# A fused normalize, convolve and project block on one core: how early products, weight rows and the low-rank preparation are ordered

## The chip, the cores and the metric

The kernel runs on one core of a Trainium2 chip. The core has TensorE (PE in the profile, its weight loads PEld), VectorE (DVE), ScalarE (ACT), GpSimd (POOL) and SyncE (SP), which here only issues transfers. Each engine works through its own instruction list in order. The metric is the device time of one execution in microseconds (us); the median of three runs is given.

## The reference

The input x has 4 x 1024 rows of 2048 numbers. A small vector c per batch gives, through a 2048 x 12288 weight, six rows per batch: shift, scale and gate for each of two halves.

```
mod = (silu(c) @ wmod).reshape(4, 6, 1, -1)        # sa, ca, ga, sb, cb, gb
h = layernorm(x) * (1 + ca) + sa
x = x + ga' * (causal_conv(h, K) + D * h)           # K: 2048 taps from a 64-state model
h = layernorm(x) * (1 + cb) + sb
x = x + gb' * (h @ W.T + bias + sum_e w_e * (h @ A_e.T) @ B_e.T)
```

The gates ga', gb' keep their sign and are at least 0.25 in size. The convolution runs along the 2048 features of a row. It is linear in h, so the convolution of the shift sa is the same for every row of a batch and can be added afterwards.

## The kernel before, in words

**Stages.** The 4096 rows are 32 row tiles of 128. In the first phase (to about 880 us) each row tile is loaded (conv_load), normalized, transposed, split into two f16 parts and multiplied with a Toeplitz form of K (conv_prep, conv_mm). In the second phase (from about 880 us) 16 units of 256 rows are multiplied with the merged weight, by a Strassen-like scheme of seven products (ffn_unit, L745). The merged weight W + low-rank part is made during the first phase: prep_lora scales the low-rank factors A and B and splits B into lbh and lbl; merge, eight times, makes the low-rank products lps (L481), adds them to W on VectorE (L483) and writes the pieces to DRAM.

**Modulation.** wmod is read as six sections of 16 weight rows, each row 1 MB (mod_load, L312), each followed by four matmuls of 512 columns into one PSUM bank (mod_mm, L317; named modps). Section 1 (scale) comes first, then 0 (shift), then 2 (gate); sections 4, 3 and 5 come later, among the merges. Sections 1 and 0 alternate between pools of two and three buffers, section 2 has three buffers.

**Early tiles.** Tiles 0 and 1 are transposed without the shift, and the products of tiles 0 to 2 (EARLY = 3) are made before the gate exists. The generator rows issues the weight rows of sections 0 and 2 between these products; pace is told the columns of each group of three products and takes a row for every ROWC of them. The convolved shift is made by shift_conv (16 small f32 matmuls, gsp) and added to tiles 0 and 1 by shift_add (L409, L415): 16 matmuls against the identity (in two passes each, 32 records) put it on all partitions, four at a time. When the gate is there, gate_tile spreads it over the partitions (gps L669, gat L670), and conv_late (L645, L646) gates the three early tiles on VectorE; conv_post stores them (L651) and takes the sums for the second normalization (ScalarE, L655).

**Order.** The program text is traced by a framework that places instructions on each engine by its own estimate of when they are ready; a block under tc.issue_after(ins) is queued behind ins on that instruction's engine. From tile 3 on, PLAN lists at which points of a tile the normalization of the next tile (N), its statistics (T, F), the storing of the last (P) and steps of other work (S) are traced. A step takes one piece of the generator rest, which yields the pieces of mer (prep_lora, then the merges) and, after every second piece, one row of the modulation sections left. In the kernel before, the first piece, which is the whole of prep_lora, is taken before tile 3, and further steps start at tile R0 = 5, nine per tile:

```
    stats(EARLY + 1)
    nxt = prep(EARLY + 1)
    take(nxt, 1)
    next(fill)
    post = None
```

Buffers that matter: y has three buffers (EARLY), the transposed pieces t two, the transposes in PSUM (tp) two banks, the products five banks; one buffer, tagged we, holds in turn the factor A (la), the factor B (lb) and the weight tile of a merge.

Of the kernel before, what the change touches and what calls it, by code (L numbers as in the profile page):

```python
# [1 line left out]

# [10 lines left out]
F32 = mybir.dt.float32  # L13
# [6 lines left out]
MUL, ADD, SUB = ALU.mult, ALU.add, ALU.subtract  # L20
# [4 lines left out]
P = 128  # L25
D = 2048
NB = 4
NC = D // P
# [6 lines left out]
class Net:  # L35
# [354 lines left out]
    def shift_conv(self, pool):  # L390

        nc, v = self.nc, self.nc.vector
        sa = pool.tile([P, NC], F32, tag="sae", name="sae")
        v.tensor_scalar(sa, self.sa[:, :, 0], self.es, self.hinv[:, 0:1], MUL, MUL)
        ps = self.tps.tile([P, NC], F32, tag="t", name="gsp")
        for m in range(NC):
            nc.tensor.matmul(
                ps[:, m:NC], self.kb[:, ds(P * m, P)], sa[:, 0 : NC - m],
                start=(m == 0), stop=(m == NC - 1), skip_group_check=True,
            )  # L400
        self.gsc = self.kpool.tile([P, NC], F32, tag="gsc", name="gsc")
        v.tensor_copy(self.gsc, ps)

    def shift_add(self, ys):
        nc, v = self.nc, self.nc.vector
        for q in range(4):
            ps = self.tps.tile([P, 4, P], F32, tag="t", name="gsb")
            for c in range(4):
                nc.tensor.matmul(  # L409
                    ps[:, c], self.gsc[:, 4 * q + c : 4 * q + c + 1].to_broadcast([P, P]), self.ident,  # L410
                    start=(c == 0), stop=(c == 3), skip_group_check=True,
                )
            for y in ys:
                sl = ds(512 * q, 512)
                v.tensor_tensor(y[:, sl], y[:, sl], ps.rearrange("p c t -> p (c t)"), ADD)  # L415

    def prep_lora(self, pool, tmp):
        nc, v, io = self.nc, self.nc.vector, self.io
        ws = pool.tile([P, 2, 2], F32, tag="lws", name="lws")  # L420
        for i, n in enumerate(("coeffs", "scales")):
            x = io[n]
            for k in range(2):
                src = bass.AP(tensor=x.tensor, offset=x.offset + 8 * k, ap=[[1, 8], [0, 16], [1, 1]])
                nc.sync.dma_start(out=ws[:, i, k : k + 1], in_=src)
        a = tmp.tile([P, 2, D], F32, tag="we", name="la")
        nc.sync.dma_start(out=a, in_=io["A"].rearrange("c p k h d -> p c k (h d)"))

        am = pool.tile([P, 2], F32, tag="lam", name="lam")
        av = a.rearrange("p k d -> p (k d)").rearrange("p (c k d) -> p k c d", c=HC, k=2)  # L430
        for k in range(2):
            nc.scalar.activation(av[:, k], av[:, k], AF.Square, accum_out=am[:, k : k + 1])
        nc.scalar.activation(am, am, AF.Sqrt)
        sa, ia = self.pow2(pool, am, 2, "lsa")
        wt = pool.tile([P, 2], F32, tag="lwt", name="lwt")
        v.tensor_tensor(wt, ws[:, 0, :], ws[:, 1, :], MUL)
        v.tensor_tensor(wt, wt, ia, MUL)
        self.lsa = sa
        b = tmp.tile([P, 2, D], F32, tag="we", name="lb")
        nc.scalar.dma_start(out=b, in_=io["BfT"].rearrange("(k p) o -> p k o", p=P))  # L440
        b4 = pool.tile([P, 4], F32, tag="lb4", name="lb4")
        for k in range(2):
            nc.scalar.activation(b[:, k], b[:, k], AF.Copy, scale=wt[:, k : k + 1])
            for h in range(2):
                j = tmp.tile([P, 1024], F32, tag="wct", name="lsq")
                i = 2 * k + h
                nc.scalar.activation(j, b[:, k, ds(1024 * h, 1024)], AF.Square, accum_out=b4[:, i : i + 1])
        bm = pool.tile([P, 1], F32, tag="lbm", name="lbm")
        v.tensor_reduce(bm, b4, AX.X, ADD)
        nc.scalar.activation(bm, bm, AF.Sqrt)  # L450
        sb, self.linv = self.pow2(self.cst, self.allmax(pool, bm, 1, "lbm"), 1, "lsb")
        self.bh = pool.tile([P, 2, D], F16, tag="lbh", name="lbh")
        self.bl = pool.tile([P, 2, D], F16, tag="lbl", name="lbl")
        for k in range(2):
            nc.scalar.activation(b[:, k], b[:, k], AF.Copy, scale=sb)
            nc.scalar.copy(self.bh[:, k], b[:, k])
            v.tensor_tensor(self.bl[:, k], b[:, k], self.bh[:, k], SUB)
        self.winv = self.const("winv", [P, NC])
        self.wcd = self.dram.tile([2, 7, P, HC, 2, 512], F16, tag="wcd", name="wcd")
# [128 lines left out]
                v.tensor_tensor(lo[:, sl], src, hi[:, sl], SUB)  # L588
            yield

    def conv_mm(self, pl, hs, x, tick, early, pace=lambda n: None):
        nc, v = self.nc, self.nc.vector
        hc, hs = hs
        y = pl["y"].tile([P, D], F32, tag="y", name="y")
        yv = y.rearrange("p (j e t) -> p j e t", e=2, t=P)
        if not early:
            gv = self.gat.rearrange("p (j e t) -> p j e t", e=2, t=P)
        sums = pl["sm"].tile([P, 2], F32, tag="sums", name="sums")

        def family(ps, f, q, first):  # L600
            pf = ps.rearrange("p j t -> p (j t)")
            last = 4 * q + 3
            for i in range(last + 1):
                o = P * max(0, i - 4 * q)
                k0 = P * max(0, 4 * q - i)
                for x, z in ((0, 0), (0, 1), (1, 0)):
                    h = hs[x][:, i] if f == 0 else hc[x][:, 2 * i + 2 - f]
                    nc.tensor.matmul(  # L608
                        pf[:, o:512], h, self.kf[f][z][:, ds(k0, 512 - o)],
                        start=first, stop=(i == last and (x, z) == (1, 0)), skip_group_check=True,  # L610
                    )
                    first = False
                if i == 3 and q == 1:
                    tick()
                pace(3 * (512 - o))

        for q in range(2):
            jj = slice(4 * q, 4 * q + 4)
            pa = self.acc.tile([P, 4, P], F32, tag="a", name="ya")
            family(pa, 0, q, True)  # L620
            qs = pl["t"].tile([P, 4, P], F32, tag="qs", name="qs")
            nc.scalar.copy(qs, pa)  # L622
            tick()
            pb = self.acc.tile([P, 4, P], F32, tag="a", name="yb")
            family(pb, 2, q, True)
            v.tensor_tensor(yv[:, jj, 1, :], pb, qs, ADD)
            if not early:
                v.tensor_tensor(yv[:, jj, 1, :], yv[:, jj, 1, :], gv[:, jj, 1, :], MUL)
            tick()
            family(pa, 1, q, False)  # L630
            sl = ds(1024 * q, 1024)
            if early:
                nc.scalar.copy(yv[:, jj, 0, :], pa)
            else:
                v.tensor_tensor(yv[:, jj, 0, :], pa, gv[:, jj, 0, :], MUL)  # L635
                v.scalar_tensor_tensor(y[:, sl], y[:, sl], 1.0, x[:, sl], MUL, ADD, accum_out=sums[:, q : q + 1])  # L636
            tick()
        return y, sums
# [169 lines left out]
LPLAN = ("LL", "LL", "LL", "LL", "L", "0", "")  # L808
R0 = 5
WM, WMS = 3, 2  # L810
ROWC = 3700
EARLY = 3
X0 = 11
LEFT0 = 30
# [12 lines left out]
def net(ctx: ExitStack, tc: tile.TileContext, io):  # L827
    nc = tc.nc
    k = Net(ctx, tc, io)
# [10 lines left out]
    pl = {}  # L840
# [25 lines left out]
        yield  # L866

    def merges():
        with tc.issue_after(k.lastw.ins):
            k.prep_lora(pl["lora"], pl["mrg"])  # L870
        yield
        for c in range(HC):
            yield from k.merge(pl["lora"], pl["mrg"], c)

    mer = merges()

    def take(g, n):
        for _ in range(n):
            next(g, None)
# [10 lines left out]
    xs, hs, sts, ys = {}, {}, {}, {}  # L890
# [14 lines left out]
    n = 0  # L905
# [19 lines left out]
    def pace(n):  # L925

        cols[0] += n
        while cols[0] >= ROWC:
            cols[0] -= ROWC
            take(rows, 1)  # L930

    for r in range(2):
        load(r + 2)
# [1 line left out]
    stats(2)  # L935
    take(prep(2), 9)
    k.shift_conv(msm)
    k.shift_add([ys[r][0] for r in range(2)])
    st.close()
    for name in ("lora", "mrg"):  # L940
        pl[name] = pool(right, "p1" + name, 1, "right")
# [15 lines left out]
    fill = rest()  # L957
    p2l = ExitStack()
    pr, wc, lf = {}, {}, {}
# [21 lines left out]
    def next_left(u):  # L981
# [2 lines left out]
        lf[u] = {}  # L984
        return k.left(pr, u, lf[u])

    def step():
        if r >= R0 and "w" not in pr and next(fill, 0) == 0:
            early()

    stats(3)
# [12 lines left out]
    stats(EARLY + 1)  # L1004
    nxt = prep(EARLY + 1)
    take(nxt, 1)
    next(fill)
    post = None
    for r in range(EARLY, 32):
        if EARLY + 2 < r + 2 < 32:  # L1010
# [5 lines left out]
        if r == LEFT0:  # L1016
            while "w" not in pr:
                step()
            lgen = next_left(0)
# [19 lines left out]
        y = k.conv_mm(pl, hs.pop(r), xs[r], tick, False)  # L1039
# [12 lines left out]
    for q in range(2):  # L1052
# [5 lines left out]
        for u in range(NU):  # L1058
            b = u // 4
            if u % 4 == 0:  # L1060
                ts_ = []
                for i in range(2):
                    t = pr["g"].tile([P, 2, 512], F32, tag=f"gb{i}", name=f"gb{i}")
# [76 lines left out]
```

## Time and profile before

| | |
|---|---|
| median of 3 runs | 2149.5 us (2147.16 to 2152.45) |
| the profiled execution | 2147.28 us, of which span 2145.5 us |
| TensorE busy | 2077.9 us, 97% of the span |
| VectorE, ScalarE, GpSimd busy | 1309.7, 927.8, 5.1 us |
| mean granted TensorE clock | 0.986 |
| moved by DMA | 483.05 MB, mean 225 GB/s |

The span runs from the first to the last instruction. In the lists of the profile each row is a slice or stretch of it; busy time of an engine in a stretch can be compared with the stretch's length. A wait is named by who waited and which instruction was the last to end before it could go on; a wait on several signals carries only one name. A matmul of 512 f16 columns shows as 0.38 us but the next can start 0.216 us later. f32 matmuls are two records each.

### The profile page before, as it was taken

To read this page: it belongs to the slowest core of one execution; us is meant where nothing else is said; L and a number is where in the kernel's file an instruction comes from. 1 tells how busy PE (TensorE), PEld (TensorE's weight loads), DVE (VectorE), ACT (ScalarE), POOL (GpSimd) and SP (SyncE) were. 2 spreads that over 40 slices of the span, in tenths; PEclk is the share of its full clock that TensorE was granted. 3 is DMA by queue.
4 is the path that set the end of the run, shared out by engine and by line. 5 is a ranking of instruction groups with operands and counts; after the bars stand their busy time and mean duration, and the time that the engine had idled before them with its cause. 6 is when DMAs were issued, how large, how long until landed. Compare 5 with 4: busy or idle time off the path is not lost.

```text
span 2145.5 us, 28479 instructions
## 1 busy us (share of the span) xinstructions
PE 2077.9 (97%) x11144; PEld 1027.8 (48%) x11144; DVE 1309.7 (61%) x2356; ACT 927.8 (43%) x1697; POOL 5.1 (0%) x16
## 2 busy tenths in 40 slices
PE   6997899999999999999999999999999999999998
PEld 2343455545545555554545545545444444444444
DVE  6636888998989999666565565565433323332323
ACT  1344776677757777655554454455200000000000
POOL 0000000000000000000000000000000000000000
PEclk8998899999999999999999999999999999999999
DMA  9979457786777554297465565564794545555542
GB/s 395 359 248 342 178 193 280 283 309 253 280 282 285 187 177 167 104 377 276 175 246 192 182 241 186 197 240 180 269 353 164 185 157 165 170 164 166 176 157 69
DMA packets 127061, 483.05 MB, mean 225 GB/s; under 512 B 13577, under 2 KB 13721, under 8 KB 95951
## 3 DMA queue, kind: packets, MB, share of 16 engines
q1 hardware_dynamic: 126192, 477.55, 61.1%
q10 hardware_dynamic: 526, 2.63, 0.4%
q8 instruction: 87, 1.43, 0.3%
q0 software_dynamic: 208, 1.06, 0.1%
q14 instruction: 48, 0.39, 0.1%
HBM read 325.89 MB, written 155.30 MB: 224 GB/s over the span
## 4 chain that ended last, share of the span: by engine, by line
PE 65%; DVE 13%; ACT 8%; issue 2%; DMA 2%; DVEq 0%; ACTq 0%
PE fZ L745 23%; PE fX L745 15%; PE fY L745 15%; PE ya L608 5%; PE tp L695 3%; PE yb L608 2%; ACT t L577 2%; DVE wch L509 2%; ACT x L655 2%; DVE st L535 2%; DVE y L636 1%; DVE hc L588 1%; ACT we L500 1%; PE lps L481 1%; DVE n L552 1%
## 5 line engine op out<-in xcount | busy, mean ns | idle before, releaser
L745 PEld LDWEIGHTS <-lf 128*128 128x128 f16 x5376 | 526.0, 98 | 620.5 <-issue 0.9
L745 PE MATMUL fZ<-w,lf 128*128 128x512 f16 x2304 | 514.1, 379 | 0.6 <-ACT p L753 0.6
L745 PE MATMUL fY<-w,lf 128*128 128x512 f16 x1536 | 342.1, 379 | 0.0
L745 PE MATMUL fX<-w,lf 128*128 128x512 f16 x1536 | 342.1, 379 | 0.0
L608 PEld LDWEIGHTS <-hc 128*128 128x128 f16 x2304 | 216.1, 98 | 204.0 <-issue 38.8
L763 DVE TENSOR_TENSOR xo<-xo,gb 128x512 f32<-128x512 f32 x128 | 87.6, 689 | 235.1 <-DMA xo<-x1d 222.5
L608 PE MATMUL ya<-kh,hc 128*128 128x512 f16 (+3 forms) x768 | 191.3, 327 | 5.5 <-ACT qs L622 5.1
L608 PE MATMUL ya<-kh,hs 128*128 128x512 f16 (+3 forms) x768 | 194.0, 328 | 0.9 <-DVE kh L284 0.6
L608 PE MATMUL yb<-kh,hc 128*128 128x512 f16 (+3 forms) x768 | 191.7, 327 | 2.1 <-DVE we L483 1.2
L577 ACT ACTIVATE t<-tp,sa,ca 128x128 f32<-128x128 f32 x480 | 186.4, 468 | 12.4 <-PE tp L573 12.1
L753 ACT COPY p<-fZ 128x512 f32<-128x512 f32 x64 | 37.3, 583 | 293.1 <-PE fZ L745 275.3
L608 PEld LDWEIGHTS <-hs 128*128 128x128 f16 x1152 | 107.2, 98 | 108.6 <-issue 31.4
L697 ACT ACTIVATE gt<-tp,sb,cb 128x256 f32<-128x256 f32 x256 | 125.0, 576 | 62.5 <-PE tp L695 60.9
L753 ACT COPY p<-fX 128x512 f32<-128x512 f32 x32 | 18.8, 586 | 305.8 <-PE fX L745 241.7
L317 PE MATMUL modps<-wm,sct 128*32 128x512 f32 x768 | 115.2, 660 | 19.9 <-DMA wm<-in_wmod 12.6
L608 PE MATMUL ya<-kl,hs 128*128 128x512 f16 (+3 forms) x384 | 125.7, 327 | 1.9 <-DVE kl L285 1.9
L608 PE MATMUL ya<-kl,hc 128*128 128x512 f16 (+3 forms) x384 | 125.6, 327 | 0.0
L608 PE MATMUL yb<-kl,hc 128*128 128x512 f16 (+3 forms) x384 | 125.5, 327 | 0.0
L573 PE MATMUL tp<-ident,n 128*128 128x128 f32 x512 | 80.7, 283 | 28.4 <-ACT t L577 16.0
L768 DVE TENSOR_TENSOR fin<-fX,gb 128x512 f32<-128x512 f32 x32 | 22.1, 691 | 127.1 <-PE fX L745 127.0
L588 DVE TENSOR_TENSOR hc<-t,hc 128x512 f16<-128x512 f32 x128 | 87.5, 683 | 12.0 <-ACT hc L587 11.8
L481 PE MATMUL lps<-lbh,lac 128*128 128x512 f16 x256 | 86.1, 379 | 0.2 <-DVE y L635 0.2
(262 smaller groups left out, 2222.9 us busy)
## 6 DMA issues: line engine op xcount, KB each, us to landing
wm<-in_wmod SPq DMA_DIRECT2D x96, 1024.0 KB
lfd<-lf SPq DMA_DIRECT2D x112, 512.0 KB
lf<-lfd SPq DMA_DIRECT2D x112, 512.0 KB
x<-in_x SPq DMA_DIRECT2D x32, 1024.0 KB
x1d<-y SPq DMA_DIRECT2D x32, 1024.0 KB
x<-x1d SPq DMA_DIRECT2D x32, 1024.0 KB
xo<-x1d SPq DMA_DIRECT2D x128, 256.0 KB
out<-xo SPq DMA_DIRECT2D x128, 256.0 KB
```

Source lines behind the costliest of these rows:

```text
L317: self.last = self.nc.tensor.matmul(self.modps[32 * g : 32 * g + 32, :], self.sct[:, j].rearrange("p r b -> p (r b)"), w[:, ds(512 * g, 512)],
L481: nc.tensor.matmul(ps, la[:, x, k, h], y[:, k, osl], start=(n == 0), stop=(n == 5))
L509: v.tensor_tensor(hl[:, :, 1, :], tv, hl[:, :, 0, :], SUB)
L573: nc.tensor.transpose(tp[:, k], n[:, ds(P * (c0 + k), P)], self.ident)
L577: nc.scalar.activation(t[:, k], tp[:, k], AF.Identity, bias=self.sa[:, c, b : b + 1], scale=self.ca[:, c, b : b + 1],)
L588: v.tensor_tensor(lo[:, sl], src, hi[:, sl], SUB)
L608: nc.tensor.matmul(pf[:, o:512], h, self.kf[f][z][:, ds(k0, 512 - o)], start=first, stop=(i == last and (x, z) == (1, 0)), skip_group_chec ...
L695: nc.tensor.transpose(tp[:, c, r], xs[r][:, ds(P * (c0 + c), P)], self.ident)
L697: nc.scalar.activation(t[:, c0 + c], tp[:, c], AF.Identity, bias=self.sb[:, c0 + c, b : b + 1], scale=self.cb[:, c0 + c, b : b + 1],)
L745: nc.tensor.matmul(ps[name], lf[i][:, k, x, :], wc[i][k // 4][:, k % 4, y, :], start=(first and n == 0), stop=(n == 3 * HC - 1), skip_grou ...
L753: nc.scalar.copy(t, ps[name])
L763: v.tensor_tensor(x, x, self.gbias[:, h], ADD)
```

## The change

1. conv_mm: a group of three products is now traced inside the block that pace returns, and pace returns tc.issue_after(k.last.ins), where k.last is the last matmul of the weight rows so far. So each group of an early tile stands behind the weight row that was due before it. For tile 3 and later pace is an empty block. ROWC goes from 3700 to 3000 columns.
2. shift_conv now copies the 128 x 16 result, transposes it to 16 x 128, copies it and stores it in DRAM; shift_add reads it back on all partitions by one DMA of 1 MB into the buffer of the gate tile, both on GpSimd's queue, and adds it to each tile with one VectorE instruction over 2048 columns.
3. prep_lora has seven yields. With the modulation rows between, it takes the first piece (before tile 3) and nine steps; in tiles 3 and 4 every second step is now taken. The first piece is queued behind the last weight row's load.

```
-        self.gsc = self.kpool.tile([P, NC], F32, tag="gsc", name="gsc")
-        v.tensor_copy(self.gsc, ps)
-    def shift_add(self, ys):
-        for q in range(4):
-            ps = self.tps.tile([P, 4, P], F32, tag="t", name="gsb")
-            for c in range(4):
-                nc.tensor.matmul(ps[:, c], self.gsc[:, 4*q+c : 4*q+c+1].to_broadcast([P, P]), self.ident, ...)
-            for y in ys:
-                v.tensor_tensor(y[:, sl], y[:, sl], ps.rearrange("p c t -> p (c t)"), ADD)
+        col = pool.tile([P, NC], F32, tag="gsc", name="gsc")
+        v.tensor_copy(col, ps)
+        pt = self.tps.tile([NC, P], F32, tag="t", name="gst")
+        nc.tensor.transpose(pt, col, self.ident)
+        row = pool.tile([NC, P], F32, tag="gsr", name="gsr")
+        v.tensor_copy(row, pt)
+        self.gsd = self.dram.tile([NC, P], F32, tag="gsd", name="gsd")
+        nc.gpsimd.dma_start(out=self.gsd, in_=row)
+    def shift_add(self, pool, ys):
+        g = pool.tile([P, D], F32, tag="gat", name="gsb")
+        self.nc.gpsimd.dma_start(out=g, in_=self.gsd.rearrange("c t -> (c t)").partition_broadcast(P))
+        for y in ys:
+            self.nc.vector.tensor_tensor(y, y, g, ADD)
...
     def prep_lora(self, pool, tmp):
         nc.sync.dma_start(out=a, in_=io["A"].rearrange("c p k h d -> p c k (h d)"))
+        yield
...
         nc.scalar.activation(am, am, AF.Sqrt)
+        yield
...
         nc.scalar.dma_start(out=b, in_=io["BfT"].rearrange("(k p) o -> p k o", p=P))
+        yield
...
+        yield
         bm = pool.tile([P, 1], F32, tag="lbm", name="lbm")
         v.tensor_reduce(bm, b4, AX.X, ADD)
         nc.scalar.activation(bm, bm, AF.Sqrt)
+        yield
...
             nc.scalar.copy(self.bh[:, k], b[:, k])
+            yield
...
-    def conv_mm(self, pl, hs, x, tick, early, pace=lambda n: None):
+    def conv_mm(self, pl, hs, x, tick, early, pace=lambda n: nullcontext()):
-                for x, z in ((0, 0), (0, 1), (1, 0)):
+                with pace(3 * (512 - o)):
+                    for x, z in ((0, 0), (0, 1), (1, 0)):
...
-                pace(3 * (512 - o))
...
-ROWC = 3700
+ROWC = 3000
...
     def merges():
-        with tc.issue_after(k.lastw.ins):
-            k.prep_lora(pl["lora"], pl["mrg"])
-        yield
+        yield from k.prep_lora(pl["lora"], pl["mrg"])
...
     def pace(n):
             take(rows, 1)
+        return tc.issue_after(k.last.ins)
...
+    calls = [0]
     def step():
-        if r >= R0 and "w" not in pr and next(fill, 0) == 0:
+        calls[0] += 1
+        if r < R0 and calls[0] % 2:
+            return
+        if "w" not in pr and next(fill, 0) == 0:
             early()
...
-    next(fill)
+    with tc.issue_after(k.lastw.ins):
+        next(fill)
```

## The prediction

> **What bounds the kernel now.** I read the busy shares and the slices first, then the busy time by stretch, then waits and chain inside the worst stretch, then TensorE's instructions there. From the page of the kernel before:
>
> ```profile
> PE 2077.9 (97%) x11144; PEld 1027.8 (48%) x11144; DVE 1309.7 (61%) x2356; ACT 927.8 (43%) x1697; POOL 5.1 (0%) x16
> PE   6997899999999999999999999999999999999998
> DVE  6636888998989999666565565565433323332323
> PEclk8998899999999999999999999999999999999999
> ```
>
> TensorE fills the span; 67.6 us of it are idle, mostly in slices 1 and 4 to 5. So only idle time or the lower clock of those slices can be won. By stretch (length, busy PE, PEld, DVE, ACT, POOL, clock, DMA share, GB/s):
>
> ```profile
> 132.00:144.00 12.00, 12.00 (x78) 8.78 (x81) 5.15 (x12) 3.65 (x9) 0.00 (x0) 0.72 0.44 153
> 144.00:171.00 27.00, 27.00 (x182) 11.51 (x177) 10.53 (x20) 10.49 (x26) 0.00 (x0) 1.00 0.89 298
> 171.00:202.00 31.00, 26.87 (x152) 12.41 (x151) 22.79 (x49) 12.76 (x18) 0.00 (x0) 0.94 0.93 354
> 202.00:227.00 25.00, 5.97 (x29) 3.25 (x27) 20.89 (x52) 22.28 (x32) 0.36 (x1) 0.58 0.86 332
> 227.00:252.00 25.00, 25.00 (x152) 14.74 (x151) 23.20 (x57) 17.86 (x46) 0.00 (x0) 0.94 0.44 169
> 252.00:880.00 628.00, 614.25 (x3797) 328.13 (x3796) 562.67 (x1181) 444.02 (x920) 0.42 (x1) 1.00 0.64 236
> ```
>
> From 202 to 227 TensorE works 6 us of 25, at a clock of 0.58, while VectorE and ScalarE are full. TensorE in it, with the idle time before each piece:
>
> ```profile
> 202.17 0.22 PE L608 MATMUL ya<-kh,hc 128*128 128x128 f16 x1
> 213.38 1.97 PE L573 MATMUL tp<-ident,n 128*128 128x128 f32 x8 [10.99 <-DVE lsb_i L54]
> 216.10 1.93 PE L317 MATMUL modps<-wm,sct 128*32 128x512 f32 x8 [0.75 <-DMA wm<-in_wmod]
> 224.52 1.11 PE L573 MATMUL tp<-ident,n 128*128 128x128 f32 x4 [6.49 <-ACT t L577]
> ```
>
> The first wait is for row tile 4's normalized n (L552 runs 211.99 to 213.33; lsb_i is the last VectorE name before it). The second is for ScalarE to take transposes out of PSUM, and the chain says what ScalarE did instead:
>
> ```profile
> 215.70 3.79 ACT lb L455 x2
> 219.49 3.59 ACT lbh L456 x2
> 223.07 1.74 ACT t L577 x5
> ```
>
> So the low-rank preparation stands in front of tile 4's preparation. VectorE is behind for another reason: the late gating of tiles 0 to 2 (L645, L646) starts only at 180.56.
>
> **What the Trainium skill says.** "TensorE: Matmul & The Clock Gate", Part 1, gives half clock after an idle window of about 3.4 us; the trace agrees (a 384-column product takes 0.32 us of issue at 138, 0.165 normally). "DMA: Bandwidth & Descriptors", Issuing engines are not separate DMA queues: transfers from all engines share the same 16 DMA engines; so the new broadcast competes with the weight rows. The same page, Anatomy of one DMA, has about 2.0 us fixed plus bytes over 436 GB/s, 4.4 us for 1 MB; under load this trace has 5.2 us for the 8 KB kd store and 10.0 us for the 1 MB kb load on GpSimd's queue, and I use those. "Perfetto Trace Analysis", Optimization Strategy, advises interleaving regimes with different bounds, which is what the spread preparation is.
>
> **The change part by part.** Instruction orders are those of the two built programs. I compare three places.
>
> *(a) Up to the end of tile 2's products.* Before, from 64.3 us: 3 tiles x 41,472 columns x 0.2158/512 us = 52.4; 31 weight rows x 1.00 = 31.0; 48 transposes x 0.115 = 5.5; the shift's convolution gsp 4.7; its broadcast gsb 0.57 + 1.66 + 1.9 = 4.1 (32 passes); 0.5 else. Sum 98.2, waits 1.9 + 1.2, and 4 for half clock from 132 to 144: 169.6; the trace has it at 171.4. The new form takes gsb away and adds one transpose (0.2): -4. VectorE does two adds of 2,048 (2 x 2.3, as lbl) where it did eight of 512 (2 x 2.48): nothing.
>
> A row every 3,072 columns costs TensorE 1.3 + 1.0 = 2.3 us, the transfer 2.58 at the 407 GB/s of the stretch from 20 to 40 us. The row order is strict now, so rows could starve TensorE. Between the 64th us and the last row are 31 rows, 2 x tiles and the broadcast, 34 x 2.58 = 87.7, less some 2.5 rows already there: 81. TensorE needs about 88 to the same place, since transposes and gsp lie between rows: covered on average, 1 to 3 us lost to local order. If the cover is gone it is 0.3 us a row, 9 in all.
>
> The broadcast's wait: behind its add on VectorE stand tile 3's subtractions, behind these ScalarE's next transposes and the copy qs of tile 2, and for that TensorE's third family. Landing is 1 + 0.5 + 5.2 + 0.5 + 10.0 = 17 us after the transpose, the copy is done at 23; TensorE arrives there after 8 rows, 23,000 columns and 16 transposes = 19.5, or 23.5 with the half clock seen at this place. Bounds: 0 to 4 us; I take 1. Tile 2's products end at 167 to 169 against 171.4.
>
> *(b) The gate.* The last weight row comes 2,304 + 29,952 columns = 13.6 us before that end, where before it came after the start of tile 3. The gate's 3.5 us of VectorE and Abs are hidden in it. The broadcast of the gate (gps, 4.0) follows directly, so the first late gating starts near 170, not 180.56: 10.5 us earlier.
>
> *(c) From there to the first merge product.* VectorE's work, counted from the order: 17 of 1,024 (1.22), 15 of 512 (0.61), 10 hc and 10 hs (0.60, 0.34), 11 sm (0.34), 16 stats (0.62), 3 n (1.26), 2 gate halves still to come (0.76), 2 lbl (2.25), some 60 small (7): about 70 us. The same count of before gives 64, and the trace 71.0 (180.56 to 251.57), so 7 were waits. After: 170 + 70 + 3 to 7 = 243 to 247, with 6 us of work done more than before had: worth 251.57 + 6 - 245 = 12 us.
>
> TensorE over the same piece: tile 3 ends near 191 with its three rows; n of tile 4 comes at 197.5 (VectorE's sum up to it), an idle 6 us; transposes are no longer behind L455 and L456, and tile 4's products start near 203 instead of 227.5. They run, fed by VectorE, to 224; tile 5's first family, transposes and three rows to 229.5. Then the moved wait: the first low-rank product needs lbh, whose two scalings (1.99 each) and casts (1.89) wait for the scale at about 229 on VectorE, so lbh comes at 234.8: 5.3 us idle. TensorE is at 239.5 where before it was at 257, with two weight rows (2 us) more behind it: 17.5 us, less some 4 for half clock after the idle: 13.5. ScalarE's 19.5 us of preparation (2 x 1.9, 2 x 1.99, 4 x 1.06, 2 x 1.99, 2 x 1.89) are neither fewer nor more; they lie under tiles 3 and 4.
>
> What is late next is the merge's weight tile: it shares the buffer of lb, so its load can't start before lbl is done at about 239; it lands 5 to 7 us later, when VectorE gets there (246). Price without that cover: what it is late. From tile 5 on there are 182 steps left in both programs, in the same order, so what is gained is kept; VectorE at 90% there (562.67 of 628) can hold back a part, which is why I go no higher.
>
> Sum: 12 by VectorE, 13.5 by TensorE, and a little recovered: 14 us. The profiled execution took 2147.28, span 2145.5 and 1.8 around; less 14 it is 2133.3. The median of the runs lies 2.2 higher: 2135.5.
>
> **Rivals.** *The larger gain:* lbh is in time, or the clock doesn't fall at 191: 14 + 5 + 4 = 23 us, 2126. For it: ScalarE has waits in (c) that my sum fills; against: VectorE's count.
>
> *The stall only moves:* ScalarE has 12 us of its own a tile and 10 of preparation against some 19.5 us of TensorE a tile; if in-order waits cost as much as the 25 us block, only gsb's 4 us remain: 2145. For it: VectorE is full either way; against: 10.5 us of earlier start are VectorE time that lies idle before (it works 10.53 of the 27 us from 144 to 171).
>
> *Slower:* strict rows make the early stage wait for transfers. Place: rows 19 to 48, with three buffers in the last sixteen. 31 MB at 300 GB/s would take 108 us instead of 88, all of it on TensorE: 14 - 20 = 6 lost, 2155.5, more if slower; it decides below about 370 GB/s. For it: 298 and 310 GB/s are all this stage shows; against: TensorE asked for no more then, and 0 to 60 us ran at 395 to 407.
>
> **How the numbers follow.** Forecast 0.58 (alone 2130 to 2142), larger gain 0.17, moved stall 0.14, slower 0.11. A measurement tells 0.3%, 6.4 us, from no change. Faster: 0.58 + 0.17 = 0.75; same 0.14; slower 0.11. The range 2124 to 2149 reaches to the moved stall and the larger gain, and leaves out the slower case and the far end of the larger gain; it holds the broadcast's 0 to 4, the rows' 0 to 9 and the moved wait's 0 to 10.
>
> **What would show it.** The 25 us stretch should shrink to 6 or so idle before tile 4's transposes, with their releaser n and not L455; no wait of the weight rows above 3 us in sum between 64 and 150; first late gating near 170; a new wait of a few us of the first low-rank product for lbh. It is wrong if weight rows wait for their DMA at every row, if TensorE waits on qs while VectorE waits for gsb, or if the first merge comes near 250 as before.

## The result and the profile after

The changed kernel takes 2142.6 us in the median of six runs (2140.33 to 2145.74), beside 2151.5 us for the kernel before on the same chip (now six runs, with the three of the table above among them): a ratio of 0.9960, 95% interval 0.9946 to 0.9974. It is 8.9 us faster, where 14 were forecast.

The two profiled executions show less of this than the medians do. The one after took 2145.74 us (span 2143.8), the longest of its six; the one before, 2147.28 us, is among the shortest of its own. The two traces differ by 1.5 us. They are good for what waits for what, and the size is left to the medians.

The busy shares and TensorE's slices, from the page of the changed kernel:

```profile
PE 2080.1 (97%) x11113; PEld 1026.8 (48%) x11113; DVE 1308.9 (61%) x2351; ACT 927.3 (43%) x1697; POOL 6.2 (0%) x18
...
PE   6897999999999999999999999999999999999998
```

TensorE's idle time is 63.7 us against 67.6. Its busy time rose by 2.2 us, although the 32 records of the shift's broadcast (4.1 us) are gone. The gap in slices 4 and 5 is smaller, not closed. The same stretches as before (length, busy PE, PEld, DVE, ACT, POOL, clock, DMA share, GB/s):

```profile
132.00:144.00 12.00, 11.64 (x67) 6.68 (x65) 3.60 (x9) 4.06 (x11) 1.09 (x2) 0.72 0.62 225
144.00:171.00 27.00, 26.55 (x180) 11.84 (x177) 13.36 (x21) 10.89 (x26) 0.00 (x0) 1.00 0.89 325
171.00:202.00 31.00, 22.99 (x112) 11.39 (x110) 16.87 (x32) 16.12 (x21) 0.00 (x0) 0.89 0.68 244
202.00:227.00 25.00, 20.45 (x124) 11.40 (x124) 24.56 (x62) 16.75 (x37) 0.00 (x0) 0.86 0.92 342
227.00:252.00 25.00, 22.55 (x143) 12.18 (x142) 23.50 (x58) 21.01 (x40) 0.35 (x1) 0.93 0.48 177
252.00:880.00 628.00, 615.55 (x3774) 328.14 (x3773) 564.33 (x1185) 442.14 (x918) 0.41 (x1) 1.00 0.65 237
```

From 202 to 227 TensorE now works 20.45 us instead of 5.97. But from 171 to 202 it lost 3.9 us, from 227 to 252 another 2.4, and VectorE, which I had wanted full from 171 on, works 16.87 us there instead of 22.79. TensorE's waits in that piece, from its list of instructions:

```profile
191.86 0.59 PE L614 MATMUL ya<-kh,hc 128*128 128x512 f16 x1 [6.75 <-ACT qs L627]
214.20 1.97 PE L578 MATMUL tp<-ident,n 128*128 128x128 f32 x8 [3.28 <-DVE n L557]
...
218.55 0.61 PE L614 MATMUL ya<-kh,hs 128*128 128x512 f16 x1 [0.52 <-ACT hs L592]
247.11 0.38 PE L486 MATMUL lps<-lbh,lac 128*128 128x512 f16 x1 [2.45 <-ACT lbh L460]
```

The transposes of tile 4 wait 3.28 us for n, no longer behind the scaling and casting of B. In their place stands a wait of 6.75 us inside tile 3's products, for ScalarE's copy out of PSUM (qs). The chain of waits from 157 us says why:

```profile
157.68 15.88 DMA la<-in_A
173.66 3.90 ACT la L432 x4
177.60 11.66 DMA lb<-in_BfT
189.34 2.01 ACT lb L445
191.38 0.45 ACT qs L627
191.86 7.67 PE ya L614 x33
```

A's load, the squares of A, B's load and the first scaling of B follow each other, and tile 3's copy stands behind that scaling in ScalarE's list. ScalarE sits idle until B has landed, and from 185.1 us on TensorE with it. (L445 was L443 in the kernel before, where it stood behind the stores' squares and didn't wait.)

### The profile page after: what moved, and what is told of

It is laid out like the page before. It is cut to its first block, busy times and chain, and to the rows that moved or that the text cites. A ratio compares the mean times of both kernels' runs of the same rounds, so it can differ in the third digit from the quotient of the medians.

```text
span 2143.8 us, 28420 instructions
## 1 busy us (share of the span) xinstructions
PE 2080.1 (97%) x11113; PEld 1026.8 (48%) x11113; DVE 1308.9 (61%) x2351; ACT 927.3 (43%) x1697; POOL 6.2 (0%) x18
## 4 chain that ended last, share of the span: by engine, by line
PE 70%; DVE 13%; DMA 8%; ACT 6%; issue 2%; SPq 0%; ACTq 0%; DVEq 0%
PE fZ L750 23%; PE fY L750 15%; PE fX L750 15%; PE ya L614 6%; PE yb L614 3%; PE tp L700 2%; PE modps L317 2%; DMA wm<-in_wmod 2%; PE lps L486 2%; ACT x L660 2%; DVE hc L593 1%; DVE wch L514 1%; ACT t L582 1%; DVE st L540 1%; DVE y L641 1%
## 5 line engine op out<-in xcount | busy, mean ns | idle before, releaser
L593 DVE TENSOR_TENSOR hc<-t,hc 128x512 f16<-128x512 f32 x128 | 87.4, 683 | 10.5 <-ACT hc L592 9.9
```

## The experiments

Two theories stood at the start; the forecast had put the gain down to both of their causes. **Theory A**: the preparation in nine steps is what gains. **Theory B**: the denser, strict weight rows gain, by an earlier gate, and the nine steps only move the wait. Times are medians, with that of the kernel before on the same chip beside them; "alone" means on the kernel before. The ratio is the one on record, with its 95% interval. It isn't the quotient of the two medians; the two differ by up to 0.0012, so a difference between two ratios that is smaller than this says nothing.

**1. The nine steps alone.** The kernel before with the seven yields of prep_lora, the step counter and the queueing of the first piece:

```
-        with tc.issue_after(k.lastw.ins):
-            k.prep_lora(pl["lora"], pl["mrg"])
-        yield
+        yield from k.prep_lora(pl["lora"], pl["mrg"])
```

> The kernel before with the low-rank preparation in nine steps alone. Theory A (the preparation standing in front of tile 4 was the cost, and spreading it is the gain): 8 to 12 us faster than before, with the idle time of TensorE ahead of tile 4's transposes down from 11 + 6.5 us to under 8. Theory B (the gain comes from the earlier gate, so from the denser rows; the preparation only moves its wait): within 3 us of before, with a new wait on ScalarE for lb's transfer of some 10 us in the place of the old one.

Measured: 2150.0 us beside 2149.1, ratio 1.0002 (0.9992 to 1.0012). No gain. What the nine steps were to do does happen: tile 4's first product starts at 215.3 us instead of 227.3. But the preparation is only pushed back: the first scaling of B goes from 201.9 to 218.4, its last cast ends at 255.1 instead of 223.1, and the first low-rank product comes at 253.4, after the 250.1 of before. The wait for B's transfer that Theory B expected is not there: that scaling starts without waiting. TensorE's waits from 171 to 310 us in this kernel:

```profile
PE tp L579 <- DVE r_v L69: 9.3, 1, 9.3
...
PE lps L487 <- ACT lbh L461: 1.8, 1, 1.8
```

TensorE's idle time falls from 67.6 to 62.6 us, its busy time rises from 2077.9 to 2082.2; where those 4.3 us of slower work lie I did not settle.

**2. The pacing alone.** pace returns the queueing block, ROWC 3000:

```
-ROWC = 3700
+ROWC = 3000
     def pace(n):
             take(rows, 1)
+        return tc.issue_after(k.last.ins)
```

> The kernel before with early products behind their weight rows and a row every 3000 columns, alone. Theory A: nothing gained, 0 to 4 us slower, since TensorE waits on rows (about 3 us more idle between 80 and 160 us than before, as in the changed kernel) and the gate that comes earlier meets the undivided preparation on ScalarE. Theory B: 6 to 9 us faster, the late gating starting near 170 instead of 180.6.

Measured: 2141.7 us beside 2149.1, ratio 0.9959 (0.9945 to 0.9974): as much as the whole change gains, by this part alone. The time is Theory B's, its reason isn't: late gating starts at 179.5, not near 170. So what the pacing does had to be asked anew (experiments 5 to 7).

**3. The shift's broadcast through DRAM alone.**

```
-            for c in range(4):
-                nc.tensor.matmul(ps[:, c], self.gsc[:, ...].to_broadcast([P, P]), self.ident, ...)
+        self.nc.gpsimd.dma_start(out=g, in_=self.gsd.rearrange("c t -> (c t)").partition_broadcast(P))
```

> The kernel before with the shift's convolution broadcast through DRAM alone. If TensorE's 32 passes (4.1 us) were on the path: 3 to 4 us faster. If VectorE and ScalarE set the end of this stage (the 25 us block comes at the same time): under 1 us. If the wait for the broadcast holds up tile 3's preparation: slower by 1 to 3 us, with a wait of VectorE for gsb.

Measured: 2152.6 us beside 2149.1, ratio 1.0013 (1.0005 to 1.0021): slightly slower. TensorE's waits from 171 to 252 us:

```profile
PE tp L572 <- DVE lsb_i L52: 19.4, 1, 19.4
PE modps L317 <- DMA wm<-in_wmod: 4.1, 1, 4.1
```

The wait at tile 4's transposes was 11.0 us in the kernel before and is 19.4 here: TensorE gets there with less to do and waits for the same n (213.8 against 212.0). All its waits in this stretch sum to 28.7 us against 23.3 before, so the 4.1 us saved ahead of a wait that VectorE and ScalarE set went into waiting. Why it is 5.4 and not 4.1 stays open; the wait of VectorE for the broadcast (gsb) that could have made it slower does not appear.

**4. The changed kernel without the wait for B.** The scaling of B queued behind tile 3's last copy out of PSUM:

```
+            with self.tc.issue_after(self.lastqs.ins):
                 nc.scalar.activation(b[:, k], b[:, k], AF.Copy, scale=wt[:, k : k + 1])
```

> The changed kernel with the scaling of lb queued behind tile 3's last copy qs on ScalarE, so that the wait for lb's transfer (10.7 us) no longer stands in front of the copies that TensorE needs and the sums that VectorE needs. Theory A: the waits of 6.75 us on TensorE and 6.7 us on VectorE go, 4 to 7 us faster than the changed kernel, 13 to 16 faster than before. Rival C (VectorE's queue sets this stage in any case): within 2 us of the changed kernel, 7 to 11 us faster than before.

Measured: 2134.2 us beside 2149.1, ratio 0.9924 (0.9909 to 0.9939), some 8 us below the changed kernel. The 6.75 us wait is gone, the first scaling of B runs at 189.94 without waiting, n of tile 4 comes at 203.5 instead of 212.8 and the first low-rank product at 241.2 instead of 247.1. So the wait for B costs the changed kernel about 8 us, more than the 5 us that are missing from the forecast. Late gating starts at 178.66 in this kernel, only 1.9 us earlier than in the kernel before: its gain of some 15 us came without the early gate that the forecast had counted on.

**5. The pacing with a late preparation.** If the pacing gains because A's squares start earlier, holding them back must take the gain away. The squares get a bias of zero that VectorE makes after the gate; the rows stay early:

```
+            self.zero = pool.tile([P, 1], F32, tag="zero", name="zero")
+            v.tensor_scalar(self.zero, t[:, D - 1 : D], 0.0, None, MUL)
-            nc.scalar.activation(av[:, k], av[:, k], AF.Square, accum_out=am[:, k : k + 1])
+            nc.scalar.activation(av[:, k], av[:, k], AF.Square, bias=self.zero, accum_out=am[:, k : k + 1])
```

> The early products' new pacing alone, but the first squaring of the low-rank preparation on ScalarE is given an operand that VectorE makes only after the gate (one more instruction of 128x1, about 0.15 us): the weight rows stay early, the chain of the preparation (squares of A, load of B, scalings, casts) starts about 10 us later, as in the kernel before. Theory P (the pacing's gain is that the last weight row frees ScalarE's preparation 10 us sooner, so that tile 4's transposes are taken out sooner): the gain is gone, 2147 to 2151 us, with the squaring of A at 181 to 184. Theory Q (the gain is in TensorE's rows or in the gate themselves): 2140 to 2144, as with the pacing alone (2141.7).

Measured: 2149.8 us beside 2150.3, ratio 0.9994 (0.9986 to 1.0003): the gain is gone. Compare ScalarE's list in the kernel with the pacing alone,

```profile
171.94 1.92 ACT L432 ACTIVATE la<-la 128x2048 f32<-128x2048 f32 x1 [1.90 <-DMA laf<-in_A]
...
207.27 3.91 ACT L455 ACTIVATE lb<-lb,lsb_s 128x2048 f32<-128x2048 f32 x2 [0.86 <-DVE lsb_s L55]
211.07 3.69 ACT L456 CAST lbh<-lb 128x2048 f16<-128x2048 f32 x2
214.66 1.50 ACT L577 ACTIVATE t<-tp,sa,ca 128x128 f32<-128x128 f32 x4
```

with that of this kernel:

```profile
184.70 2.00 ACT L432 ACTIVATE la<-la,zero 128x2048 f32<-128x2048 f32 x1 [0.79 <-DVE zero L672]
...
217.48 3.90 ACT L455 ACTIVATE lb<-lb,lsb_s 128x2048 f32<-128x2048 f32 x2
221.26 3.70 ACT L456 CAST lbh<-lb 128x2048 f16<-128x2048 f32 x2
225.68 1.51 ACT L577 ACTIVATE t<-tp,sa,ca 128x128 f32<-128x128 f32 x4
```

With early squares the 7.6 us of scaling and casting end at 214.8, where tile 4's transposed pieces begin; TensorE waits for them there:

```profile
216.21 1.12 PE L573 MATMUL tp<-ident,n 128*128 128x128 f32 x4 [4.93 <-ACT t L577]
```

Held back, they lie in the middle of these pieces, and the first scalings of B (201.3 to 205.3) lie in front of tile 3's last copy: TensorE waits 9.2 us for that copy and 4.3 us for the pieces. The squares start at 184.7 here, 3.2 us later than in the kernel before; so the run shows that a late preparation takes the gain away, and not yet that an early one makes it. One thing stays open: TensorE idles 16.3 us from 180 to 252 here, 6 less than in the kernel before, without being faster; it started its products 1.9 us later and idles 4.5 us more between 310 and 880.

**6. Strict rows, but not denser.** ROWC stays 3700.

> The kernel before with the weight rows queued strictly behind their products, but still one row for every 3,700 columns: the last row then stands in front of 114,432 columns of products (127,872 in the kernel before, 92,160 with one row for every 3,000), about 6 us earlier in time than before, where the pacing alone had 10. Theory P (the time of the last row sets the start of the low-rank preparation, and that the gain): a part of the pacing's gain, 2143.5 to 2147 us. Theory R (strictness or the gate's place at tile 2's end is what counts, both are here): the whole gain, 2140 to 2143.

Measured: 2141.6 us beside 2148.5, ratio 0.9970 (0.9960 to 0.9981). The time is Theory R's. My premise failed: the last row comes earlier in the order of the list but not in time (its copy runs at 175.7 us, 174.1 before), and A's squares start at 181.45, as in the kernel before (181.50). So an early row is not needed for the gain. What ScalarE does about tile 4, from its list in this kernel:

```profile
212.91 0.44 ACT L577 ACTIVATE t<-tp,sa,ca 128x128 f32<-128x128 f32 x1
...
216.91 1.18 ACT L577 ACTIVATE t<-tp,sa,ca 128x128 f32<-128x128 f32 x3
217.95 3.92 ACT L455 ACTIVATE lb<-lb,lsb_s 128x2048 f32<-128x2048 f32 x2
```

Nine transposed pieces are taken out before the scaling of B starts; in the kernel before the first came at 222.98, behind it. Strictness (with the gate's place at tile 2's end) cannot be the cause by itself either, for experiment 5 has both and no gain. An earlier gate is not the cause: late gating starts at 183.17 here, later than the 180.56 of before.

What the gaining kernels (2 and 6) share, and the others (before and 5) lack, is that tile 4's products start earlier (221.0 and 217.1 us, against 227.3 and 225.8), and with them the first low-rank product (243.1 and 244.4, against 250.1 and 249.3). They come to it by different orders on ScalarE. With the pacing alone the block of scaling and casting still stands in front of tile 4's pieces, but it ends at 214.8 instead of 223.1; with strict rows nine pieces stand before it. In neither does TensorE wait long for tile 3's last copy (3.5 us and not at all), as it does in experiment 5 (9.2). That is read from four lists. No run moved that block alone, so which of these orders gains, and how much, is not shown.

**7. Rows denser still.** ROWC 2400, pacing alone.

> The pacing alone with one row for every 2,400 columns: TensorE then asks for a row about every 2.0 us on average, the transfers give one in 2.6 to 2.8 us. The rival of my forecast (strict rows starve TensorE): waits of the rows sum to 8 to 14 us, the last row is hardly earlier than with 3,000, and the time is 2145 to 2152. Theory P without starvation: the last row comes 5 us earlier again and the time is 2136 to 2140.

Measured: 2145.2 us beside 2148.5, ratio 0.9982 (0.9974 to 0.9989). The time is the rival's, the reason only in part. TensorE's waits from 64 to 171 us:

```profile
PE modps L317 <- DMA wm<-in_wmod: 4.0, 7, 1.0
...
PE tp L573 <- DVE y L415: 3.1, 1, 3.1
```

The rows wait 4.0 us in sum and not 8 to 14, and the last one is 5 us earlier, as Theory P said (copy at 159.1 against 164.2). But the end of tile 2's products comes at 188.7 instead of 176.7, and late gating at 193.8 instead of 179.5. VectorE has to wait 5.55 us for the tiny loads of the scale columns (lws) there, the shift's adds stand behind that, and tile 3's transposes wait for them; then TensorE is at a clock of 0.71 from 170 to 180. A row for every 3000 and for every 3700 columns gain the same within their intervals (0.9959 and 0.9970); 2400 seems to gain less (0.9982), with an interval that still meets theirs.

**8. The gate inside tile 2's products.** The changed kernel, with gate_tile, and the late gating, storing and next loads of tiles 0 and 1, traced as soon as the gate's rows are complete, and the product of the scale columns (lwt) queued behind the gate:

```
             take(rows, 1)
+        if hasattr(k, "gas") and not hasattr(k, "gat"):
+            gate()
         return tc.issue_after(k.last.ins)
...
+        with self.tc.issue_after(self.lastgat.ins):
+            v.tensor_tensor(wt, ws[:, 0, :], ws[:, 1, :], MUL)
```

> The changed kernel with the gate's broadcast, and the late gating of tiles 0 and 1, put in as soon as the gate's weight rows are complete, inside tile 2's products, and not behind their end; the product of the two scale columns (lwt) is queued behind the gate. Theory G (my forecast's step b: the late gating's start sets tile 4's input): late gating starts at 165 to 170 and not at 180.1, and 4 to 8 us come off: 2135 to 2139. Theory H (the low-rank preparation on ScalarE sets it, the gate has slack): 2141 to 2145, as the changed kernel.

Measured: 2137.3 us beside 2150.3, ratio 0.9930 (0.9914 to 0.9946). Theory G's figure. From VectorE's list of this kernel:

```profile
164.71 1.28 DVE L651 SCALAR_TENSOR_TENSOR y<-y,rat,gat 128x1024 f32<-128x1024 f32 x1
...
197.48 1.34 DVE L558 TENSOR_SCALAR n<-x,mv,rs 128x2048 f32<-128x2048 f32 x1
```

Late gating starts 15.4 us earlier than in the changed kernel, and tile 4's n comes 15.3 us earlier. But the edit also changed ScalarE's order: B's scaling now runs at 193.46, behind tile 3's copies (189.64). So this run doesn't part the early gate from the removed wait for B.

**9. Both.** The gate inside tile 2's products, and B's scaling queued as in 4.

> The gate inside tile 2's products together with the scaling of B behind tile 3's last copy out of PSUM. Theory G: 4 to 8 us below the version with the scaling alone (2134.2): 2126 to 2130. Theory H: within 2 us of it, 2132 to 2136.

Measured: 2135.1 us beside 2150.3, ratio 0.9919 (0.9903 to 0.9935), within the interval of experiment 4 (0.9924). That is what Theory H expected. The two edits don't add up: each takes away the same wait, and what the early gate brings beyond it (tile 4's n at 197.7 against 203.5 in experiment 4) isn't there at the end. In its place TensorE waits 3.2 us for VectorE's split pieces (hs) and 2.4 for lbh. This and experiment 4 beat both kernels, by 0.7 to 0.8% against the kernel before.

**10 to 12. The parts put together.** First, pacing and nine steps without the DRAM broadcast:

> Pacing and nine-step preparation, the shift's small products left as before. If the preparation in nine steps adds nothing once the rows are early: within 2 us of the pacing alone, 2140 to 2144. If it adds what the version without the wait for B shows (7 us): 2133 to 2137. If its wait for B costs as in the changed kernel: 2143 to 2147.

Measured: 2142.6 us beside 2148.5, ratio 0.9969 (0.9957 to 0.9981): nothing beyond the pacing alone. This is also the changed kernel less the broadcast. B's scaling waits 5.0 us for its transfer here, TensorE only 1.4 for tile 3's copy but 9.0 for tile 4's n; so the place of B's scaling need not show as a wait for that copy. Then the same with B's scaling moved as in 4, so that only the broadcast differs from experiment 4:

> The changed kernel without the shift's broadcast through DRAM (the shift's 32 small products on TensorE stay as before), and with the scaling of B behind tile 3's last copy. If the broadcast costs here what it costs alone (2.8 us, 0.13%): 2131 to 2132. If it saves its 4 us of TensorE here: 2137 to 2139. If it does nothing here: 2133 to 2135.

Measured: 2138.5 us beside 2150.3, ratio 0.9934 (0.9918 to 0.9950), against 2134.2 and 0.9924 with the broadcast: the intervals overlap. Last, that with the gate's edit too, to be held against experiment 9:

> As the version with the gate inside tile 2's products and B's scaling moved (2135.1), but with the shift's 32 small products on TensorE as before in place of the broadcast through DRAM. If the broadcast saves its TensorE time here (the pair without the early gate suggested 4 us with wide intervals): 2137 to 2140. If it does nothing: 2133.5 to 2136.5. If it costs as alone: 2131 to 2133.

Measured: 2138.5 us beside 2148.5, ratio 0.9954 (0.9942 to 0.9966), against 2135.1 and 0.9919 (0.9903 to 0.9935) with the broadcast: these do not overlap. TensorE's busy time is 2081.0 against 2076.9 us, which is the 4.1 us of the 32 small products. So the broadcast, which loses 0.1% alone, gains in this pair, where B's scaling is out of the way. By the medians it is 3.4 us (0.16%), about its TensorE time; the ratios give 0.35%, twice what that time can explain, and the two kernels ran on different chips.

## Why the prediction was right or wrong

The direction and the range hold: 2142.6 us lies within 2124 to 2149, but outside the likeliest case's own 2130 to 2142, and nearer to the rival "the stall only moves" (2145) than to 2135.5. By cause it is that rival too, in good part: the 25 us stall shrank and a new one of 6.75 us came ahead of it. That the range holds is in part luck: of the three places below, (a) and (b) went another way than forecast. It is luck in part, too, that experiment 4, with the new wait gone, lands 1.3 us from the forecast's 2135.5, for it has no early gate either.

**(a) Up to the end of tile 2's products: wrong.** Forecast 167 to 169, found 176.05 (before 171.4), where gps begins. Against the kernel before, four terms make up 3.8 of the 4.6 us more. The first product started at 68.84 instead of 65.94, with the same instructions ahead of it: 2.9 us, which I had not thought of. Over all these kernels this start lies between 65.8 and 69.5, so this term need not come from the change. A row that before came after tile 2's end is now in front of it: 1.0, which my sum left out. Idle time from 64 to 176 grew by 4.0, of which the rows' waits are 3.4 (I had 1 to 3). The removed broadcast gave 4.1, as said. That part went well: store and load landed in 1.6 and 6.8 us where I had 5.2 and 10.0 (the Trainium skill, "DMA: Bandwidth & Descriptors", Anatomy of one DMA, has a formula that makes an estimate of 4.4 for a load of this size, so this trace lies between), and the adds were never waited for.

**(b) The gate 10.5 us earlier: did not come.** By its numbers the forecast's 170 was the end of tile 2's products and, directly after it, the first half of the gate's broadcast; so it failed with (a). The last row does come earlier, and the gate is ready after the last VectorE instruction on it, at 169.8. But its broadcast stands behind tile 2's last product in TensorE's list:

```profile
168.27 0.16 DVE L437 TENSOR_TENSOR lwt<-lws 128x2 f32<-128x2 f32 x1 [5.22 <-DMA lws<-in_scales]
...
169.13 0.69 DVE L347 SCALAR_TENSOR_TENSOR mg<-mg,mg 128x512 f32<-128x512 f32 x1
...
178.58 1.52 DVE L675 TENSOR_SCALAR gat<-gps,fs_i,ks_i 128x512 f32<-128x512 f32 x2
180.14 1.28 DVE L650 SCALAR_TENSOR_TENSOR y<-y,rat,gat 128x1024 f32<-128x1024 f32 x1
```

The broadcast begins at 176.05, and late gating follows at 180.14, against 180.56 before. These 4.1 us were 2.9 before: VectorE's list now holds the scale of A (lsa) in front of gat, and that waits for A's squares until 177.8. The 5.22 us wait for lws in this list is new as well, but hidden: tile 2's products end later. Where the gate really is put early (experiment 8), tile 4's n comes at 197.48, the 197.5 of the forecast. Experiment 9, held against 4, shows what that is worth at the end once B's scaling is out of the way: nothing.

**(c) The preparation under tiles 3 and 4: the step that cost the difference.** That ScalarE's 19.5 us of preparation (the terms add to 19.8) lie under tiles 3 and 4 counted its busy time and left out that one of its instructions waits for a transfer. The first scaling of B waits 10.68 us, and ScalarE's list holds tile 3's copy behind it: 6.75 us of TensorE, and 6.67 us of VectorE behind the store's squares. Experiment 4 puts the price at about 8 us. The two waits that (c) named came, and were smaller: tile 4's transposes wait for n and not for the scaling (3.3 us; 6 forecast), the low-rank product waits for lbh (2.45 us; 5.3 forecast). Tile 4's products start at 218.6 (203 forecast, 227.3 before).

After the new wait of 6.75 us the products of 512 columns start 0.42 us apart where 0.216 is usual; that agrees with the half clock that the Trainium skill, "TensorE: Matmul & The Clock Gate", Part 1, gives after an idle window. The place that the forecast took for it, at 138 us, is not such a case: TensorE's records show no idle time from 132 to 144, and the half clock there (0.50 from 136 to 141) comes right after 4.7 us of 32 products of 16 columns (gsp).

**Which part gains: wrong.** I gave the gain to the earlier gate that the pacing was to bring and to the nine steps. The pacing alone has the whole gain (0.9959), and not by the gate, which is hardly earlier in experiment 2 and later in 6. That the place of ScalarE's preparation decides fits experiment 5, where holding it back takes the gain away, but which part of the order does it is not shown. The nine steps alone gain nothing (1.0002), and the broadcast alone loses a little (1.0013).

**The slower rival: did not come.** It was to decide below about 370 GB/s. From 100 to 132 us the rate was 369 GB/s, and the rows waited 3.4 us in all. Even with a row for every 2,400 columns they waited 4.0.

## What to carry to other kernels

Work of an idle engine isn't hidden by fitting its busy time under another stage: look through its list for the instruction that waits for a transfer, and for what stands behind it. Time saved ahead of a wait that another engine sets may go into that wait: the same broadcast cost 0.1% alone, and saved 3.4 us by the medians in one pair of kernels where B's scaling was out of the way. Before a gate or a buffer is called early, find the product in the list behind which it stands.

## What the runs showed of the hardware

Small loads can be late among large ones: the scale columns (0.5 KB each) are issued from 154.9 to 157.6 us, between 1 MB weight rows and A's 2 MB, and are used at 168.3, at the end of a wait of 5.2 us for them (0.45 us with the pacing alone); A's and B's loads of 2 MB take 15.9 and 11.7 us in the chain, 132 and 180 GB/s, while the stretch from 100 to 132 us moves 369. On GpSimd's queue the 1 MB load of the broadcast took 6.8 us and the 8 KB store before it 1.6, where the loads and stores of the same sizes that the forecast went by (kb and kd, in the kernel before) had taken 10.0 and 5.2: a duration taken from one place of a trace was off by a factor of about three at another.
